# A recurrent layer: half of its products as bf16 sums, the other products in one bank

## The chip, the cores and the metric

One core of one Trainium2 chip runs the kernel; the other cores are idle. The metric is device time of the whole program in microseconds, the median of several runs. TensorE (PE in the profile; PEld is its weight load) multiplies matrices into PSUM; VectorE (DVE), ScalarE (ACT) and GpSimd (POOL) do the rest, and SyncE (SP) issues most DMAs. The clock granted to TensorE is 1.000 over the whole profiled run.

## The reference

A gated recurrent layer walks over 512 steps of a sequence, for a batch of 8, with 512 inputs and 512 state units, all in fp32. Its result is added to the input.

```python
def step(h, x_t):
    fused = jax.nn.sigmoid(jnp.concatenate([x_t, h], axis=-1) @ w_W + w_b)
    hidden_state, output_state = jnp.split(fused, 2, axis=-1)
    memory_state = x_t @ wx_W + wx_b + hidden_state * (h @ wh_W + wh_b)
    h_new = output_state * h + (1.0 - output_state) * jnp.tanh(memory_state)
    return (h_new, h_new)
_, hs = jax.lax.scan(step, h0, xT)
return x + jnp.swapaxes(hs, 0, 1)
```

Below, r is `hidden_state`, z is `output_state`, and hh is `h @ wh_W + wh_b`. Each step needs three products of h (r, z, hh) and three of x (r, z, and the memory's own). The products of x do not depend on h and can be made ahead; those of h make up a loop that no step can leave.

## The kernel before

**Layout.** The 512 units are cut into 4 chunks of 128 for the contraction (index `k`) and into 4 quarters for the output (index `j`). A product of h has 8 columns of state (stationary; 32 are loaded, of which the 8 rows of the current step are used) and streams a weight slice. Quarter j of the output goes to partitions 32j to 32j+31 of a PSUM tile, so four products stand side by side. The output columns are again cut into two halves: half A is chunks 0 and 1 of the next state, half B is chunks 2 and 3.

**Steps and groups.** `GS = 4` steps form a group. The rows 8s to 8s+7 of each 32 belong to step s of the group, and the x products of all four steps are made at once. PSUM tiles exist twice, one set for each group in turn. Weights and states are fp32; an fp32 product is two TensorE instructions, each with its weight load.

**Recurrent products.** Three tiles hold them: `A` with 192 columns (hh, z and r of half A), `B` with 128 (r and hh of half B), `C` with 64 (z of half B). `ORDER = "A0 B0 A1 A2 A3 B1 B2 B3 C0 C1 C2 C3"` is the order on TensorE; the digit is the chunk of h. Bank A is complete first, so that half A can be worked on while B and C are still being written.

**x products.** From group 4 on, pairs of groups are computed with a seven-product scheme (`products`, `weight_sum`, `x_sum`), which trades an eighth of the multiplications for sums on VectorE, ScalarE and GpSimd. A piece of it follows the recurrent products in each step (`take(later, 1)`), ahead of the next step's products. The first groups use plain products (`prefill`). `spread` copies the finished x part of r, z and hh into the banks of the next group (ScalarE), and `turn_x` transposes the memory's own x part into `md1` (VectorE). The x parts already hold the biases.

**Half A, then half B.** The instructions are put on their queues in the order of the program text (a manual schedule). On VectorE, for half A: a transpose of r, of hh and of z, a very short memset that waits for the second of these, a scan `m = r * hh + x` for each of the two chunks (`memory`), and, after the transposes of r and hh of half B, the two updates (`update`, also a scan). ScalarE does sigmoid of r, sigmoid of -z, and a tanh for each chunk in between. The scan of an update works on three cells for each element of h: the old h in slot 0, tanh in slot 1, and in slot 2 again the old h, in whose place the new tile gets the new one; factors 0, -1 and sigmoid(-z) make h + (1 - z)(tanh - h) of them. A copy of the new h into slot 0 (`act(("h", ...))`) prepares the next step. The first product of the next step (A0) waits for the first update of half A, A1 for the second, A2 and A3 for those of half B.

**Output.** GpSimd adds x and the new state into `ot` (16 steps), half B first, and SP stores 256 KB every 16 steps; the last 16 steps leave in two stores, the last of 4 steps.

**Waits.** They are set by the framework from tiles and regions; `declare_no_dep` takes some away that are implied by others, `add_manual_dep` adds some.

Names the prediction uses: `mm` (L193) makes all matmuls, so all of them show as L194; `act` (L223) makes all activations (L224); transposes of r and z are L406, of hh L422; all scans are L390; additions of the output are L558.

Of the kernel before, what the change touches and what calls it, by code (L numbers as in the profile page):

```python
# [11 lines left out]
PSUM = bass.MemoryType.PSUM  # L12

# [4 lines left out]
HU = 64  # L18

DVE_FILL = 23
IDLE = 3
LAST = 4
SYNC = mybir.DependencyInfo(mybir.DependencyClass.Sync, mybir.DependencyReason.DATA)

ORDER = "A0 B0 A1 A2 A3 B1 B2 B3 C0 C1 C2 C3"

FIRST = "A0 x A1 x A2 x A3 B0 B1 B2 B3 C0 C1 C2 C3"

BANKS = {"A": 192, "B": 128, "C": 64}

HALF = 192

WIDE = 384

SUMS = ((2,), (2,), (2, 1), (2, 1), (1,), (1, 3), (3,), (3, 3))

Q01, Q23 = slice(0, 64), slice(64, 128)

COLS = slice(64, 448)

XP = {"A": slice(0, 192), "X": slice(192, 320), "C": slice(320, 384), "B": slice(384, 512)}
# [3 lines left out]
def tile_cond_rnn_residual(  # L47
# [5 lines left out]
    wa_d: bass.AP,  # L53
    wb_d: bass.AP,
    wb3_d: bass.AP,
# [4 lines left out]

# [13 lines left out]

# [47 lines left out]

# [8 lines left out]

    wa = const.tile([P, NQ, NQ, 192], F32, name="wa")
    for k in range(NQ):
        nc.sync.dma_start(out=wa[:, k], in_=wa_d[k])
    wb = const.tile([P, NQ, NQ, 192], F32, name="wb")
    nc.sync.dma_start(out=wb[:, :3], in_=wb_d)
    nc.sync.dma_start(out=wb[:, 3], in_=wb3_d)

    def wh(bank, k, j):
        return wa[:, k, j] if bank == "A" else wb[:, k, j, {"C": slice(0, 64), "B": slice(64, 192)}[bank]]  # L140
# [3 lines left out]
    def pair(n, name, rows, slots):  # L144

        return const.tile([P, 2, rows, slots], F32, name=name).rearrange("p c n s -> p n c s")

    NH = 2 * GS  # L150
    hT = [[pair(n, f"hT{n}{i}", 32, 3) for i in range(NH)] for n in "AB"]

    md0 = [[pair(n, f"md0{n}{i}", 32, 2) for i in range(2)] for n in "AB"]
    md1 = [[pair(n, f"md1{n}{i}", 32, 2) for i in range(2)] for n in "AB"]
    hd0 = [[pair(n, f"hd0{n}{i}", B, 3) for i in range(2)] for n in "AB"]
# [3 lines left out]
    nc.vector.memset(none, 0.0)  # L159

# [6 lines left out]
    for n, t_ in enumerate(hd0[0] + hd0[1] + md0[0] + md0[1] + hT[0] + hT[1]):  # L167
        (nc.vector if n < DVE_FILL else nc.gpsimd).memset(t_, 0.0)
    for t_ in hd0[0] + hd0[1]:
        nc.gpsimd.memset(t_[:, :, :, 1], -1.0)  # L170
    idle = const.tile([P, IDLE], F32, name="idle")

    tw = [const.tile([P, 2, 2, WIDE], F32, name=f"tw{n}") for n in range(4)]
    sx = [[const.tile([P, 2, GS * B], F32, name=f"sx{n}{q}") for q in range(2)] for n in range(4)]
    step_bias = const.tile([P, HALF], F32, name="stepbias")
    xs = [const.tile([P, 512], F32, name=f"xs{n}") for n in range(2)]
    u2 = const.tile([P, WIDE], F32, name="u2")
    u3 = const.tile([P, WIDE], F32, name="u3")
    both = const.tile([P, WIDE], F32, name="both")

    def state(hf, i, slot=2):

        s = i % GS
        return hT[hf][i % NH][:, B * s : B * s + B, :, slot]

    ctx.enter_context(tc.manual_schedule())
    banks = [
        {n: psum.tile([P, w], F32, name=f"{n}{q}") for n, w in BANKS.items()}
        for q in range(2)
    ]  # L190
    xps = [psum.tile([P, 512], F32, name=f"xp{q}") for q in range(2)]

    def mm(out_, lhsT, rhs, start=False):  # L193
        nc.tensor.matmul(  # L194
            out_, lhsT, rhs, start=start, stop=False, skip_group_check=True
        )


    for t_ in list(banks[0].values()) + list(banks[1].values()):
# [10 lines left out]
    for t_ in xs:  # L210
        for c_ in (slice(0, 64), slice(448, 512)):
            nc.gpsimd.tensor_copy(t_[:, c_], bias[:, c_])
    for hf in range(2):
        for slot in (0, 2):
            nc.vector.tensor_copy(
                state(hf, 0, slot), hin[:, 2 * hf : 2 * hf + 2].rearrange("p c b -> p b c")
            )

    written = {}

# [6 lines left out]

    def seed(g):  # L230

        nc.scalar.copy(xps[g % 2][:, COLS], bias[:, COLS])

    def prefill(g):

        c, t0 = divmod(g * GS, TC)
        for k in range(NQ):
            for j in range(NQ):
                mm(
                    xps[g % 2][32 * j : 32 * j + 32, 64:448],  # L240
                    x_of(c, k, t0, GS),
                    wx[:, k, j, :],
                )
            yield

    def prefill_two():
        yield from prefill(2)
        yield from prefill(3)

    def source(g):  # L250

        return xs[g % 2] if g else xps[0]

    def spread(g, names):

        for n in names:
            nc.scalar.copy(banks[g % 2][n], source(g)[:, XP[n]])

    def turn_x(g, e):

        c0 = XP["X"].start + 32 * e
        nc.vector.transpose(md1[e // 2][g % 2][:, :, e % 2, 1], source(g)[:, c0 : c0 + 32])

    def wx_of(kh, nh):
        return wx[:, 2 * kh : 2 * kh + 2, 2 * nh : 2 * nh + 2]

    def x_half(o, n, kh):

        return x_of(o // 2, slice(2 * kh, 2 * kh + 2), 8 * (o % 2) + GS * n, GS)

    def weight_sum(n, k=slice(0, 2), j=slice(0, 2)):

        a, b = [
            (wx_of(0, 1), wx_of(0, 0)),
            (wx_of(1, 1), tw[0]),
            (wx_of(1, 1), wx_of(0, 1)),
            (wx_of(1, 0), tw[1]),
        ][n]
        at = (slice(0, P), k, j)
        nc.vector.tensor_tensor(tw[n][at], a[at], b[at], ALU.subtract)  # L280

    def x_sum(o, n):

        t_ = [q[o % 2] for q in sx]
        a, b, op = [
            (x_half(o, 1, 0), x_half(o, 1, 1), ALU.add),
            (t_[0], x_half(o, 0, 0), ALU.subtract),
            (x_half(o, 0, 0), x_half(o, 1, 0), ALU.subtract),
            (x_half(o, 0, 1), t_[1], ALU.subtract),
        ][n]  # L290
        nc.gpsimd.tensor_tensor(t_[n], a, b, op)

    def products(o):

        t_ = [q[o % 2] for q in sx]
        p1 = (0, x_half(o, 0, 0), wx_of(0, 0))
        p2 = (0, x_half(o, 0, 1), wx_of(1, 0))
        p3 = (0, t_[3], wx_of(1, 1))
        p4 = (1, x_half(o, 1, 1), tw[3])
        p6 = (0, t_[1], tw[1])  # L300
        p7 = (1, t_[2], tw[2])

# [55 lines left out]
    for e in range(NQ):  # L358
        turn_x(0, e)
# [297 lines left out]
```

## Time and profile before

| | |
|---|---|
| Median of 3 runs | 1662.64 us (1661.88 to 1666.37) |
| Profiled execution, first to last instruction | 1659.2 us |
| Median less that span | 3.4 us |
| PE busy | 1647.1 us, 99% |
| PEld busy | 1484.3 us, 89% |
| DVE busy | 1298.5 us, 78% |
| ACT busy | 1106.9 us, 67% |
| POOL busy | 325.6 us, 20% |
| Chain that ended last | PE 98%, DMA 1%, DVE 1% |
| PEld waiting for the update of half A (hTA) | 107.1 us in 379 waits |
| DVE waiting for bank A | 199.3 us in 384 waits |

How to read it: rows of the groups give line, engine, operation, tile written <- tiles read, shape and count, then busy time in us and the mean in ns, then idle time of that engine just before, with what ended most of it. Rows in order of time give start, length and the same names; idle time stands in brackets. Rows of the chain give start, length, engine, tile and count. Matmul ends are modelled, and busy time of several engines overlaps.

### The profile page before, as it was taken

How to read it: one execution, taken by the hardware profiler on the slowest of the kernel's cores; microseconds unless marked ns; L12 is line 12 of the kernel's file. 1: busy time of each engine (PE TensorE's matmuls, PEld its weight loads, DVE VectorE, ACT ScalarE, POOL GpSimd, SP SyncE). 2: the span in 40 equal slices, each digit the busy share in tenths (PEclk: the TensorE clock that was granted, in tenths of full speed). 3: DMA queues.
4: the chain of work that ended last, by engine and by line, in shares of the span. 5: the costliest groups of instructions: out<-in, count | busy, mean ns of one | idle time of the engine just before them, and what ended most of it. 6: DMA issues, size and time to landing. Idle time of an engine off the chain costs nothing.

```text
span 1659.2 us, 126037 instructions
## 1 busy us (share of the span) xinstructions
PE 1647.1 (99%) x54254; PEld 1484.3 (89%) x54254; DVE 1298.5 (78%) x9702; ACT 1106.9 (67%) x5884; POOL 325.6 (20%) x1284
## 2 busy tenths in 40 slices
PE   8999999999999999999999999999999999999998
PEld 5899999999999888899999999988899999999997
DVE  6877777777777777777777777777777777777776
ACT  4666666666666666666666666666666666666665
POOL 2221121211211212112112121121121211211211
PEclk9999999999999999999999999999999999999999
DMA  4000000000000000000000000000000000000000
GB/s 180 17 5 18 17 18 18 17 6 18 17 17 18 5 18 18 18 18 5 18 18 18 18 12 10 18 17 18 18 5 18 17 18 18 5 17 11 11 11 10
DMA packets 11512, 31.16 MB, mean 19 GB/s; under 512 B 1220, under 2 KB 1732, under 8 KB 10824
## 3 DMA queue, kind: packets, MB, share of 16 engines
q1 hardware_dynamic: 10800, 22.94, 4.0%
q8 instruction: 424, 6.95, 1.8%
q14 instruction: 136, 1.11, 0.2%
q10 hardware_dynamic: 152, 0.16, 0.0%
HBM read 14.70 MB, written 8.39 MB: 14 GB/s over the span
## 4 chain that ended last, share of the span: by engine, by line
PE 98%; DMA 1%; DVE 1%; issue 0%; ACT 0%; SPq 0%
PE A L194 40%; PE B L194 26%; PE xp L194 18%; PE C L194 13%; DMA wb<-in_wb_dram 1%; DMA wx<-in_wx_dram 0%; DVE tr L406 0%; DVE m L390 0%; DVE tz L406 0%; DVE hTA L390 0%; DVE md1A L422 0%; DVE md1B L422 0%; ACT hTB L224 0%; SPq L130 0%; DVE hTB L390 0%
## 5 line engine op out<-in xcount | busy, mean ns | idle before, releaser
L194 PE MATMUL A<-wa,hTA 128*32 128x192 f32 x8176 | 555.5, 327 | 2.7 <-DVE hTA L390 2.7
L194 PE MATMUL B<-wb,hTA 128*32 128x128 f32 x8192 | 453.0, 273 | 0.9 <-DMA wb<-in_wb_dram 0.9
L194 PE MATMUL A<-wa,hTB 128*32 128x192 f32 x8176 | 446.6, 326 | 0.0
L194 PEld LDWEIGHTS A<-wa,hTA 128*32 128x32 f32 x8176 | 290.7, 122 | 128.4 <-DVE hTA L390 107.1
L558 POOL TENSOR_TENSOR ot<-xin,hTB 128x16 f32<-128x16 f32 x503 | 125.6, 250 | 1292.4 <-DVE hTB L390 1281.8
L194 PEld LDWEIGHTS B<-wb,hTA 128*32 128x32 f32 x8192 | 346.8, 122 | 10.8 <-DMA wb<-in_wb_dram 1.3
L194 PE MATMUL B<-wb,hTB 128*32 128x128 f32 x8192 | 338.6, 273 | 0.1
L194 PEld LDWEIGHTS A<-wa,hTB 128*32 128x32 f32 x8176 | 324.3, 122 | 15.5 <-DVE hTB L390 0.3
L224 ACT ACTIVATE md0A<-tr 128x16 f32<-128x16 f32 x512 | 112.3, 219 | 314.4 <-DVE tr L406 314.4
L406 DVE STREAM_TRANSPOSE tr<-A 128x64 f32<-128x64 f32 x511 | 127.7, 250 | 214.3 <-PE A L194 199.3
L194 PE MATMUL xp<-tw,sx 128*32 128x384 f32 x1984 | 274.2, 406 | 0.3 <-issue 0.3
L194 PEld LDWEIGHTS B<-wb,hTB 128*32 128x32 f32 x8192 | 261.1, 122 | 0.4 <-DMA wb<-in_wb_dram 0.4
L390 DVE TENSOR_TENSOR_SCAN hTB<-hd0B,hTB 128x24 f32<-128x24 f32 x1024 | 157.8, 195 | 100.5 <-ACT hTB L224 100.5
L194 PE MATMUL C<-wb,hTB 128*32 128x64 f32 x8192 | 230.0, 219 | 0.1
L194 PE MATMUL C<-wb,hTA 128*32 128x64 f32 x8192 | 229.1, 219 | 0.0
L194 PE MATMUL xp<-wx,xin 128*32 128x384 f32 x1056 | 210.1, 486 | 0.0
L194 PEld LDWEIGHTS C<-wb,hTA 128*32 128x32 f32 x8192 | 206.6, 122 | 0.0
L390 DVE TENSOR_TENSOR_SCAN hTA<-hd0A,hTA 128x24 f32<-128x24 f32 x1024 | 190.9, 186 | 0.0
L194 PEld LDWEIGHTS C<-wb,hTB 128*32 128x32 f32 x8192 | 179.5, 122 | 0.6 <-issue 0.4
L224 ACT ACTIVATE hd0B<-tz 128x16 f32<-128x16 f32 x512 | 115.7, 226 | 94.8 <-DVE tz L406 94.8
L224 ACT ACTIVATE hTB<-hTB 128x16 f32<-128x16 f32 x512 | 120.1, 235 | 79.2 <-DVE hTB L390 70.3
L224 ACT ACTIVATE hTA<-m 128x8 f32<-128x8 f32 x1024 | 160.8, 206 | 2.5
(98 smaller groups left out, 2710.0 us busy)
## 6 DMA issues: line engine op xcount, KB each, us to landing
xin<-in_x_dram SPq DMA_DIRECT2D x31, 256.0 KB, 3.3
out_dram<-ot SPq DMA_DIRECT2D x31, 256.0 KB, 2.1
wx<-in_wx_dram SPq DMA_DIRECT2D x4, 768.0 KB, 7.1
wa<-in_wa_dram SPq DMA_DIRECT2D x4, 384.0 KB, 9.1
wb<-in_wb_dram SPq DMA_DIRECT2D x1, 1152.0 KB
wb<-in_wb_dram SPq DMA_DIRECT2D x1, 384.0 KB, 11.2
out_dram<-ot SPq DMA_DIRECT2D x1, 192.0 KB, 2.1
head<-in_xh_dram ACTq DMA_DIRECT2D x1, 144.0 KB, 5.0
```

The source lines that it names most:

```text
L194: nc.tensor.matmul(out_, lhsT, rhs, start=start, stop=False, skip_group_check=True)
L224: inst = nc.scalar.activation(out_, in_, func, **kw).ins
L390: return nc.vector.tensor_tensor_scan(*[t_[:, :, c_].rearrange("p n c s -> p (n c s)") for t_ in (out_, d0, d1)], 0.0, ALU.mult, ALU.add,).ins
L406: inst = nc.vector.transpose(t_.rearrange("p c n -> p (c n)"), raw[n][hf]).ins
L558: return engine.tensor_tensor(ot[:, t, 2 * hf : 2 * hf + 2, :].rearrange("p c n -> p n c"), x_of(c, slice(2 * hf, 2 * hf + 2), t, 1).rearr ...
```

## The change

**Recurrent products.** One fp32 tile `M` of 256 columns holds hh, r and z of half A and r of half B. `COLS` cuts it: M0 and M1 (chunks 0, 1 of h) write all 256 columns, A2 and A3 the columns of hh and r of A, R2 and R3 those of z of A and r of B. A second tile `Z` of 128 columns holds hh and z of half B. Its products are in bf16: each fp32 weight is split before the loop into three bf16 numbers whose sum is exact (`split`), and so is each new h (`first_piece`, a ScalarE copy whose upper 16 bits serve as the first piece; `other_pieces`, two GpSimd subtractions). The three pieces of h are 24 stationary columns, the three of the weights are three products, so that 3 x 3 partial products come out as 24 rows, summed over the weights' pieces in PSUM. The three rows of each element, and a fourth with the bias, are summed later: for hh by a longer scan (five cells for each element, `SL = 5`), for z by a `tensor_reduce`. Z has a tile for each step in turn.

**Order.** `"M0 M1 Z0 A2 A3 R2 R3 Z1 Z2 Z3"`, then one chunk of the plain x products of the group after next.

**x side.** `products` and all its sums are gone; `prefill` is used throughout, 384 columns for one chunk in each step. Two groups are made ahead of the loop. `spread` copies two pieces of 128 columns for a group, `turn_x` transposes directly from `xp`.

**Others.** The copy of half B's h into slot 0 and both output additions are on GpSimd, in the order: pieces of A, addition of A, pieces of B, copy of B, addition of B. The last 16 steps leave in one store. The weights are loaded in other pieces (wzf, then wm).

```diff
-ORDER = "A0 B0 A1 A2 A3 B1 B2 B3 C0 C1 C2 C3"
-BANKS = {"A": 192, "B": 128, "C": 64}
+ORDER = "M0 M1 Z0 A2 A3 R2 R3 Z1 Z2 Z3"
+COLS = {"M": slice(0, 256), "A": slice(0, 128), "R": slice(128, 256)}
+HA, RA, ZA, RB = (slice(HU * n, HU * n + HU) for n in range(4))
+    banks = [psum.tile([P, 256], F32, name=f"M{q}") for q in range(2)]
+    zbanks = [psum.tile([P, 128], F32, name=f"Z{q}") for q in range(2)]
+    def first_piece(hf, i):
+        first_of[hf] = act(("p", hf, i % 2), pieces[hf][i % 2][:, :, :B], state(hf, i), AF.Copy)
+        after_products(first_of[hf], hf, i)
+
+    def other_pieces(hf, i):
+        t_ = pieces[hf][i % 2]
+        hi = t_.rearrange("p c n -> p (c n)").bitcast(BF16).rearrange("p (c n) -> p c n", c=2)[:, :, 1::2]
+        d = nc.gpsimd.tensor_tensor(t_[:, :, B : 2 * B], state(hf, i), high(hf, i), ALU.subtract).ins
+        after_products(d, hf, i)
+        e = nc.gpsimd.tensor_tensor(
+            t_[:, :, 2 * B : 3 * B], t_[:, :, B : 2 * B], hi[:, :, B : 2 * B], ALU.subtract
+        ).ins
+        after_products(e, hf, i)
+        tc.add_manual_dep(e, first_of[hf].name, SYNC)
+    def split(k):
+        w = wzf[:, k]
+        t_ = work.tile([P, NQ, 128], F32, tag="split", name=f"split{k}")
+        nc.scalar.copy(wzp[:, k, :, 0], w)
+        nc.vector.tensor_tensor(t_, w, wzp[:, k, :, 0], ALU.subtract)
+        nc.scalar.copy(wzp[:, k, :, 1], t_)
+        nc.vector.tensor_tensor(wzp[:, k, :, 2], t_, wzp[:, k, :, 1], ALU.subtract)
+        for n in ORDER.split():
+            bank, k = n[0], int(n[1])
+            if bank != "Z":
+                hs = hT[k // 2][i % NH][:, k % 2, :, 2]
+                for j in range(NQ):
+                    mm(ps[32 * j : 32 * j + 32, COLS[bank]], hs, wm[:, k, j, COLS[bank]])
+                continue
+            hf, q = divmod(k, 2)
+            hs = pieces[hf][i % 2].rearrange("p c n -> p (c n)").bitcast(BF16)
+            hs = hs.rearrange("p (c n) -> p c n", c=2)[:, q, 1 : 2 * ROWS : 2]
+            for p in range(NP):
+                for j in range(NQ):
+                    inst = mm(pz[32 * j : 32 * j + ROWS, :], hs, wzp[:, k, j, p], start=k == p == 0)
...
+        if g in later:
+            take(later[g], 1)
...
+        tr = turned("rA", RA)
+        act(("rA", g % 2, s), a0[:, :, rows, 1], tr, AF.Sigmoid)
+        h_done = nc.vector.transpose(a1[:, :, :, 0], ps[:, HA]).ins
+        tz = turned("zA", ZA)
+        act(("zc", 0, i % 2), hd0[0][i % 2][:, :, :, 2], tz, AF.Sigmoid, scale=-1.0)
+        inst = nc.vector.memset(idle[:, :1], 0.0).ins
+        tc.add_manual_dep(inst, h_done.name, SYNC)
+        scan_m(0, 0)
+        tr = turned("rB", RB)
+        scan_m(0, 1)
+        tanh(0, 0)
+        act(("rB", g % 2, s), b0[:, :, rows, SL - 1], tr, AF.Sigmoid)
+        tanh(0, 1)
+        nc.vector.transpose(b1[:, :2, rows, : SL - 1].rearrange("p c n s -> p c s n"), pz[:, :HU])
+        update(0, 0)
+        z_done = nc.vector.transpose(b1[:, 2:, rows, : SL - 1].rearrange("p c n s -> p c s n"), pz[:, HU:]).ins
+        tc.add_manual_dep(z_done, pool_done[i].name, SYNC)
+        update(0, 1)
+        if not last:
+            first_piece(0, i + 1)
+            other_pieces(0, i + 1)
+        scan_m(1, 0)
+        tanh(1, 0)
+        nc.vector.tensor_reduce(zB, b1[:, 2:, rows], mybir.AxisListType.X, ALU.add)
+        act(("zc", 1, i % 2), hd0[1][i % 2][:, :, :, 2], zB, AF.Sigmoid, scale=-1.0)
+        scan_m(1, 1)
+        tanh(1, 1)
+        update(1, 0)
+        update(1, 1)
+        if s == 0 and g + 1 < NG:
+            turn_x(g + 1)
+        if s in (1, 2) and g + 1 < NG:
+            spread(g + 1, "AR"[s - 1])
...
+            again(0, i + 1)
+            first_piece(1, i + 1)
+            add(0, nc.gpsimd)
+            other_pieces(1, i + 1)
+            again(1, i + 1)
+            add(1, nc.gpsimd)
+        if s == 3 and g + 3 < NG:
+            seed(g + 3)
```

`again` copies the new h into slot 0, on ScalarE for half A and on GpSimd for half B.

More of the change, by code (lines that the diff above doesn't have):

```diff
@@ L209, in tile_cond_rnn_residual, with after_products @@
     nc.vector.tensor_copy(bias, xps[0])
[L210 to L217, printed above, removed]
-    written = {}
+    for t_ in zbanks:
+        nc.vector.tensor_copy(t_[:, :HU], bias[:, 448:])
+    written = {}
+    read = set()
+    def after_products(inst, hf, i):
+        key = f"z{hf}{i % 2}"
+        if key in read:
+            tc.declare_no_dep(inst, group=key, reason="ordered through VectorE")
     def act(key, out_, in_, func, **kw):
@@ L345, in take @@
             n = None if n is None else n - 1
[L347 to L362 removed]
+    def split(k):
[5 more added lines that the diff above has]
+        nc.vector.tensor_tensor(wzp[:, k, :, 2], t_, wzp[:, k, :, 1], ALU.subtract)
+    seed(0)
+    take(prefill(0))
+    seed(1)
+    take(prefill(1))
+    spread(0, "M")
+    turn_x(0)
+    seed(2)
+    for k in range(NQ):
+        split(k)
+    later = {}
     for i in range(T):
@@ L563, in add @@
             ).ins
[L565 to L583 removed]
+        last = i == T - 1
```

435 lines of the change are left out of this document (103 added, 332 removed).

## The prediction

> **What bounds the kernel now.** I read the page first, then the chain that ended last, then the order of time in one late step.
>
> ```profile
> span 1659.2 us, 126037 instructions
> PE 1647.1 (99%) x54254; PEld 1484.3 (89%) x54254; DVE 1298.5 (78%) x9702; ACT 1106.9 (67%) x5884; POOL 325.6 (20%) x1284
> ```
> ```profile
> 803.27 0.65 PE xp L194 x8
> 803.92 0.33 PE A L194 x8
> 804.24 0.22 PE B L194 x8
> 804.46 0.97 PE A L194 x24
> 805.43 0.66 PE B L194 x24
> 806.09 0.45 PE C L194 x32
> ```
> In mid-run the chain is PE alone, and this step takes 3.28 us (803.27 to 806.54): 2.63 us of recurrent products, 0.65 us of x products. The paces behind it: 40 ns per instruction at 192 columns (0.97/24), 27.5 at 128 (0.66/24), 14 at 64 (0.45/32); an fp32 product is two instructions.
>
> ```profile
> 35.17 0.25 DVE L406 STREAM_TRANSPOSE tr<-A 128x64 f32<-128x64 f32 x1 [0.71 <-PE A L194]
> 1654.18 0.25 DVE L406 STREAM_TRANSPOSE tr<-A 128x64 f32<-128x64 f32 x1 [0.95 <-PE A L194]
> ```
> These are the first transposes of steps 4 and 511: 1619.0 us over 507 steps, 3.193 us a step, so the x share is 0.56 on average.
>
> The last steps have no x products left, and there the other limit can be seen bare: the loop through VectorE and ScalarE. First the chain view, then the order of time.
>
> ```profile
> 1649.29 0.55 PE A L194 x8
> 1649.84 0.22 PE B L194 x8
> 1650.06 1.02 PE A L194 x24
> ```
> ```profile
> 1651.10 0.25 DVE L406 STREAM_TRANSPOSE tr<-A 128x64 f32<-128x64 f32 x1 [0.94 <-PE A L194]
> ...
> 1651.40 0.21 DVE L406 STREAM_TRANSPOSE tz<-A 128x64 f32<-128x64 f32 x1
> ...
> 1651.64 0.28 DVE L390 TENSOR_TENSOR_SCAN m<-md0A,md1A 128x16 f32<-128x16 f32 x2
> ...
> 1651.83 0.23 DVE L406 STREAM_TRANSPOSE tr<-B 128x64 f32<-128x64 f32 x1
> 1651.86 0.31 ACT L224 ACTIVATE hTA<-m 128x8 f32<-128x8 f32 x2
> 1651.98 0.21 DVE L422 STREAM_TRANSPOSE md1B<-B 128x64 f32<-128x64 f32 x1
> 1652.09 0.22 ACT L224 ACTIVATE md0B<-tr 128x16 f32<-128x16 f32 x1
> 1652.11 0.20 DVE L390 TENSOR_TENSOR_SCAN hTA<-hd0A,hTA 128x24 f32<-128x24 f32 x1
> ...
> 1652.37 0.19 PEld L194 LDWEIGHTS A<-wa,hTA 128*32 128x32 f32 x8 [0.38 <-DVE hTA L390]
> ...
> 1652.38 0.17 DVE L390 TENSOR_TENSOR_SCAN hTA<-hd0A,hTA 128x24 f32<-128x24 f32 x1
> 1652.47 0.25 DVE L390 TENSOR_TENSOR_SCAN m<-md0B,md1B 128x16 f32<-128x16 f32 x2
> ```
> The loop has two arcs. On PE, from the first load of h of half A to the transpose of r of A: 1649.29 to 1651.10, 1.81 us. Its streams are 32 instructions at 40.4 ns and 8 at 27.5, 1.51 us, so 0.30 us is loading, draining and handing over. On the others, from that transpose back to PE's load: 1.27 us. Together 3.08 us, only 0.11 under the average step. PE bounds the kernel, and the loop lies just behind it. Only products before bank A is complete (A0 B0 A1 A2 A3) are in the loop; the other B, C and x products run in the shadow of the 1.27 us.
>
> **PE's own work.** Bank M has 4 chunks x 4 quarters x 256 columns: 32 fp32 instructions of 256 columns' worth, at 54 ns (40.4 x 256/192), 1.73 us. The Z products are 12 rounds of 4 bf16 instructions with 128 columns.
>
> ```profile
> L194 PE MATMUL A<-none 128*128 128x192 bf16 x2 | 0.7, 345 | 2.1 <-DVE none L159 2.1
> ```
> Two such bf16 products stand in the program and two in the row: one instruction each. One pass over 128 columns is the stream of a C product, two over 64; I take C's 14 ns, so Z0 is 12 x 14 = 0.17 us and Z1 to Z3 0.51. The row is the nearest I have; no steady bf16 row exists, and the bounds are half of it and twice (see the rivals). The plain x side is one 384-column chunk in every step, 0.65. Sum: 1.73 + 0.68 + 0.65 = 3.06, against 3.19. If PE stayed the bound, this would give 0.13 us a step. It does not stay the bound.
>
> **What the one bank does.** Before, the transpose of r of A waits for bank A alone, with B and C still to be written. Now hh, r and z of A and r of B lie in one bank. The question is whether a read of r of A must wait only for its own columns (complete after A3) or for everything written to that bank (R3).
>
> ```profile
> 12.53 0.33 ACT L257 COPY A<-xp 128x192 f32<-128x192 f32 x1
> 12.89 0.32 DVE L262 STREAM_TRANSPOSE md1A<-xp 128x32 f32<-128x32 f32 x2 [2.25 <-ACT A L257]
> ```
> Here both engines read xp, ScalarE columns 0 to 191, VectorE 192 to 255: no column in common, and yet VectorE sat idle until ScalarE's copy was over (12.86). Waits are set by bank. So I take it that the first transpose waits for R3. The Trainium skill, PSUM — Partial Sum Buffer, section "PSUM bank collisions raise a hardware error", says the same more widely: a matmul writing a bank and a VectorE read of it in the same 32 partitions collide at disjoint columns too. By that rule the column case below falls away; the row shows it for two readers only.
>
> **The new loop.** PE arc: M0 and M1, 16 x 54 ns = 0.86; Z0 0.17; A2 A3 and R2 R3, 32 x 27.5 ns = 0.88; with the 0.30 of hand-overs 2.21 us, where it was 1.81. The 0.40 more is R2 and R3 (0.44) and small differences, and all of it is in the loop.
>
> Other arc, counted from the transpose of r of A. The order up to the first update is the old one with one exchange: r of B is transposed between the two m scans, and the transpose of hh of B now reads bank Z (done 0.51 after R3, long before it is wanted at 0.88). So the first update starts at 1.01 and PE's load at 1.27 as before. The second update waits for the second tanh, which now stands behind r of B on ScalarE.
>
> ```profile
> 906.33 0.23 ACT L224 ACTIVATE hTB<-hTB 128x16 f32<-128x16 f32 x1 [0.15 <-DVE hTB L390]
> 906.47 0.32 ACT L257 COPY A<-xs 128x192 f32<-128x192 f32 x1
> ```
> r of B was transposed at 0.73 and stands one scan (0.10) earlier now, 0.63; its sigmoid starts 0.26 later (1651.83 to 1652.09), 0.89; ScalarE takes the next 0.14 behind it, 1.03; a tanh is followed by its update 0.25 later (1651.86 to 1652.11): 1.28, as before (1652.38).
>
> 2.21 + 1.27 = 3.48 us. PE has only 3.06 us of work, and Z1 to Z3 and x (1.16) end before the new load (1.27), so they are hidden.
>
> **The pieces for Z0.** A wait that did not exist: Z0 stands third in PE's order, in front of A2, and needs three pieces of half A of h: a ScalarE copy and two GpSimd subtractions one behind the other. All of PE queues behind them.
>
> ```profile
> 804.03 0.31 DVE L390 TENSOR_TENSOR_SCAN hTB<-hd0B,hTB 128x24 f32<-128x24 f32 x2 [0.20 <-ACT hTB L224]
> 804.42 0.25 POOL L558 TENSOR_TENSOR ot<-xin,hTB 128x16 f32<-128x16 f32 x1 [2.38 <-DVE hTB L390]
> ```
> ```profile
> 24.81 0.52 DVE L280 TENSOR_TENSOR tw<-wx 128x384 f32<-128x384 f32 x1
> 24.86 0.57 POOL L558 TENSOR_TENSOR ot<-head,hTB 128x16 f32<-128x16 f32 x1 [3.07 <-DVE hTB L390]
> ```
> GpSimd starts 0.08 after an update ends and takes 0.25 for 16 elements; it took 0.57 beside a VectorE operation on two SBUF tensors. The second update ends at 1.28 + 0.17 = 1.45; subtractions from 1.53 to 2.03, two hand-overs of 0.07, ready at 2.17. PE wants Z0 at 1.27 + 0.03 + 0.86 = 2.16. So even at the free price nothing is left, and the scans of half B, each on two SBUF tensors, run exactly then. They are far shorter than the 0.52 us operation, so I take 0.035 for each subtraction, near the free row: 0.07 us of stall, 3.55 us a step. Ends: 0 (3.48) and 2 x 0.32 (4.12).
>
> **Half B.** Its update is wanted by A2 at 2.16 + 0.17 + 0.07 = 2.40. Second update 1.28, a scan 0.09 later, 1.37 (1652.38 to 1652.47). That scan has 40 elements now; two of 16 take 0.25, so 0.15 until the next operation is my estimate. Then the sum of the z pieces, which has no row; priced like a transpose and its sigmoid (0.26), the sigmoid starts at 1.37 + 0.15 + 0.26 = 1.78, the update 0.25 later at 2.03, the load 0.26 later at 2.29. It is 0.1 early; a reduction slower by 0.2 would cost 0.1, a faster one gains nothing. The second half's tanh stands behind that sigmoid, 0.14 later, and A3 wants it 0.22 later than A2. What follows per step or per group (the copies of h, the spread, the seed at 0.48 us, the turned x, the two output additions) falls behind the last update, some 1 us ahead of the next first transpose; GpSimd has six operations of 0.25, 1.5 us, in 3.5.
>
> **Start and end.** SP's queue loads 3 MB of recurrent weights as before, in eight pieces for six; a step cannot start before the last of them, then or now. Four weight splits stand on ScalarE and VectorE ahead of step 0.
>
> ```profile
> L232 ACT COPY xp<-bias 128x384 f32<-128x384 f32 x3 | 1.4, 479 | 4.6 <-DVE bias L209 4.6
> 17.01 0.25 DVE L406 STREAM_TRANSPOSE tr<-xp 128x64 f32<-128x64 f32 x1 [3.62 <-PE xp L194]
> ```
> A split of 512 elements is two copies (479 x 512/384 = 0.64, taken as 0.6) and two subtractions (0.52 x 512/384 = 0.69, the row at 24.81): 2.6 us, about 2 where neighbours overlap, 8 in all from 13.1, so step 0 starts near 21.5 instead of 17.0. But steps 0 to 3 no longer carry x work for two groups (35.17 - 17.01 = 18.2 us; now 14.2 and about 1 of settling): step 4 at 36.7. The end, 5.0 us from the last first transpose, grows by a later half B and by one 256 KB store in place of 64 KB: 6.2.
>
> Sum: 36.7 + 507 x 3.55 + 6.2 = 1842.8 us of span. The profiled span stands 3.4 under the median of the runs (1659.2 to 1662.64), so **1846 us**, 11% slower. Of the 183 us, 147 are the 3.48 us loop (0.29 x 507), 35 the pieces.
>
> **The rivals.**
> Columns, not banks (not slower): the first transpose starts after A3. The PE arc loses 0.44, but z of A, second in VectorE's queue behind it, still waits for R3, 0.44 after, instead of being taken at 0.30, and moves all behind it by 0.14: 3.48 - 0.44 + 0.14 = 3.18; 36.7 + 1612.3 + 6.2 + 3.4 = 1659 us, no change. Pieces are then no tighter than above. It decides if the transpose of r starts before R2's stream is over. Against it speaks the xp row. Chance 0.09, split over faster and same.
>
> GpSimd slowed in full: both subtractions at 0.57. Step 4.12: 507 x 4.12 + 46.3 = 2135 us. For it, the 0.57 row; against it, that scans of 16 to 40 elements are not 0.5 us long. Full 0.07; half of it (3.8, 1973 us) 0.10.
>
> bf16 instructions at twice C's pace, 28 ns: Z0 costs 0.17 more in the loop, and Z1 to Z3 with x last 1.01 + 0.65 = 1.66 from R3's stream; PE is wanted about 1.55 after it (1.27 + 0.03 + the 0.25 to the transpose), so 0.11 more: 3.48 + 0.28 = 3.76, 1953 us. The C row, 14 ns for the same stream, speaks against it. Chance 0.08. The Trainium skill, TensorE: Matmul & The Clock Gate, section "Wait — 56ns, not 53.3ns?", has a floor of about 25 ns between starts of small matmuls. By that, as an estimate, Z0 would be 0.30 and the step 3.61, some 1877 us; the trace has 14 ns with four quarters side by side, and I go by it.
>
> PE stays the bound (3.06 a step, 1598 us): the loop would have to be 0.4 shorter than its rows. Chance 0.02.
>
> **How the numbers follow.** Forecast 1846 with 0.64, its own range 1790 (no stall, and 0.04 of shorter hand-overs) to 1900. Left out of 1780 to 1985: columns and PE-bound, 0.11, below, and the full GpSimd price, 0.07, above. Faster takes PE-bound and half of the column case, same the rest of it; 5 us, 0.3%, is about what the measurement can tell: faster 0.06, same 0.05, slower 0.89.
>
> **What would show it.** Right: the transpose of r waits for PE's R products; the load of M on hTA shows idle of some 0.1 to 0.4 us in every step; PE's busy share falls below nine tenths; chain shares of VectorE and ScalarE appear; Z0 waits for GpSimd. Wrong: first transpose before R3 is over; PE still 98% of the chain; Z rows above 14 ns per instruction; or GpSimd far from 0.25.

## The result

The changed kernel takes 1804.5 us in the median (1803.98 to 1804.84, four runs), the one before 1662.62 us beside it: ratio 1.085, 95% interval 1.084 to 1.087. The forecast was 1846 us, its range 1780 to 1985.

From the page of the kernel after: its span, the busy time of each engine, the queue that brings instructions (packets, MB, share), and the engines' shares of the chain that ended last.

```profile
span 1802.8 us, 125916 instructions
...
PE 1687.8 (94%) x53258; PEld 1123.5 (62%) x53258; DVE 1203.0 (67%) x8495; ACT 1054.2 (58%) x6025; POOL 719.2 (40%) x3600
...
q8 instruction: 416, 6.82, 1.7%
...
PE 61%; DVE 35%; issue 2%; DMA 1%; ACT 0%; SPq 0%; POOL 0%; DVEq 0%; ACTq 0%
```

Before, PE alone was 98% of the chain. Now VectorE has a third of it. PE is still shown as 94% busy, but its ends are modelled and its matmuls overlap, so this figure says little here; the idle time of the weight loads tells more. The groups of the kernel after:

```profile
L148 PEld LDWEIGHTS M<-wm,hTA 128*32 128x32 f32 x8192 | 241.8, 125 | 527.4 <-DVE hTA L286 452.4
...
L292 DVE STREAM_TRANSPOSE trA<-M 128x64 f32<-128x64 f32 x512 | 128.0, 250 | 507.8 <-PE M L148 507.8
...
L148 PEld LDWEIGHTS <-pcA 128*24 128x24 bf16 x12288 | 249.9, 92 | 130.5 <-POOL pcA L191 128.0
```

The first two rows are the loop with nothing to cover it: PE's loads stand idle 452.4 us for the update of half A (0.9 us a step), and VectorE's first transpose waits 507.8 us for PE (1.0 us a step). Before, these waits were 107.1 and 199.3 us. The third row is Z0's loads waiting for the pieces that GpSimd makes, 128.0 us. The chain through one step shows the two arcs one behind the other:

```profile
903.06 0.25 DVE trA L292
...
904.33 1.09 PE M L148 x16
905.41 0.17 PE Z L148 x12
905.58 0.92 PE M L148 x32
906.50 0.02 issue
906.52 0.25 DVE trA L292
```

From the transpose of r of A to PE's load is 1.27 us (903.06 to 904.33), from there back to the next transpose 2.19 us (to 906.52), 3.46 us together, where the average step before was 3.193. Over the whole run the first transposes and the weight splits ahead of them give the same sum (rows in order of time, kernel after):

```profile
17.33 0.69 DVE L236 TENSOR_TENSOR split<-wzf,wzp 128x512 f32<-128x512 f32 x1 [1.21 <-ACT wzp L235]
...
24.65 0.69 DVE L238 TENSOR_TENSOR wzp<-split,wzp 128x512 bf16<-128x512 f32 x1 [0.69 <-ACT wzp L237]
...
25.25 0.24 DVE L292 STREAM_TRANSPOSE trA<-M 128x64 f32<-128x64 f32 x1
...
40.16 0.25 DVE L292 STREAM_TRANSPOSE trA<-M 128x64 f32<-128x64 f32 x1 [1.10 <-PE M L148]
...
1797.05 0.25 DVE L292 STREAM_TRANSPOSE trA<-M 128x64 f32<-128x64 f32 x1 [1.10 <-PE M L148]
```

Steps 4 to 511: 1756.9 us over 507, 3.465 us each. The 0.272 us a step more than before make 138 of the 142 us that were lost.

### The profile page after: what moved, and what is told of

The parts are those of the page before. It is cut to its first block, busy times and chain, and to the rows that moved or that the text cites. A ratio compares the mean times of both kernels' runs of the same rounds, so it can differ in the third digit from the quotient of the medians.

```text
span 1802.8 us, 125916 instructions
## 1 busy us (share of the span) xinstructions
PE 1687.8 (94%) x53258; PEld 1123.5 (62%) x53258; DVE 1203.0 (67%) x8495; ACT 1054.2 (58%) x6025; POOL 719.2 (40%) x3600
## 4 chain that ended last, share of the span: by engine, by line
PE 61%; DVE 35%; issue 2%; DMA 1%; ACT 0%; SPq 0%; POOL 0%; DVEq 0%; ACTq 0%
PE M L148 57%; DVE mA L286 8%; DVE trA L292 7%; DVE md1B L333 5%; PE Z L148 5%; DVE trB L292 4%; DVE mdA L322 4%; DVE tzA L292 4%; DVE hTA L286 3%; DMA wzf<-in_wz_dram 1%; DVE idle L325 0%; DMA xin<-in_x_dram 0%; SPq L85 0%; DVE split L236 0%; ACT wzp L237 0%
## 5 line engine op out<-in xcount | busy, mean ns | idle before, releaser
L148 PE MATMUL M<-wm,hTA 128*32 128x256 f32 x8192 | 556.8, 389 | 100.6 <-DVE hTA L286 100.6
L148 PEld LDWEIGHTS M<-wm,hTA 128*32 128x32 f32 x8192 | 241.8, 125 | 527.4 <-DVE hTA L286 452.4
L148 PE MATMUL M<-wm,hTB 128*32 128x128 f32 x16384 | 540.8, 273 | 0.0
L292 DVE STREAM_TRANSPOSE trA<-M 128x64 f32<-128x64 f32 x512 | 128.0, 250 | 507.8 <-PE M L148 507.8
L189 POOL TENSOR_TENSOR pcA<-hTA 128x16 f32<-128x16 f32 x512 | 110.9, 217 | 889.5 <-DVE hTA L286 882.2
L148 PEld LDWEIGHTS M<-wm,hTB 128*32 128x32 f32 x16384 | 436.4, 122 | 0.0
L148 PE MATMUL Z<-wzp,pcA 128*24 128x128 bf16 x12288 | 359.4, 219 | 1.7 <-DVE wzp L238 1.0
L148 PEld LDWEIGHTS <-pcA 128*24 128x24 bf16 x12288 | 249.9, 92 | 130.5 <-POOL pcA L191 128.0
L148 PE MATMUL Z<-wzp,pcB 128*24 128x128 bf16 x12288 | 265.8, 219 | 2.9 <-ACT wzp L237 1.9
L286 DVE TENSOR_TENSOR_SCAN mB<-md0B,md1B 128x40 f32<-128x40 f32 x1024 | 229.0, 224 | 0.0
L173 ACT ACTIVATE hTB<-mB 128x8 f32<-128x8 f32 x1024 | 223.4, 218 | 0.4 <-DVE mB L286 0.4
L335 DVE STREAM_TRANSPOSE md1B<-Z 128x64 f32<-128x64 f32 x512 | 141.4, 276 | 0.0
L333 DVE STREAM_TRANSPOSE md1B<-Z 128x64 f32<-128x64 f32 x512 | 139.6, 273 | 0.0
## 6 DMA issues: line engine op xcount, KB each, us to landing
xin<-in_x_dram SPq DMA_DIRECT2D x1, 128.0 KB, 7.3
```

The lines of the kernel that those rows point to most:

```text
L148: return nc.tensor.matmul(out_, lhsT, rhs, start=start, stop=False, skip_group_check=True).ins
L173: inst = nc.scalar.activation(out_, in_, func, **kw).ins
L189: d = nc.gpsimd.tensor_tensor(t_[:, :, B : 2 * B], state(hf, i), high(hf, i), ALU.subtract).ins
L286: return nc.vector.tensor_tensor_scan(*[t_.rearrange("p n s -> p (n s)") for t_ in (out_, d0, d1)], 0.0, ALU.mult, ALU.add).ins
L292: nc.vector.transpose(t_.rearrange("p c n -> p (c n)"), ps[:, cols])
L333: nc.vector.transpose(b1[:, :2, rows, : SL - 1].rearrange("p c n s -> p c s n"), pz[:, :HU])
```

## The experiments

Theory: the loop with the 256-column bank in it sets the time, because the first transpose waits for R3. Rivals: PE's own work, x included; the pieces on GpSimd; half B.

**The x products.** Left out from the third group on, with their two lines:

```diff
-        if g in later:
-            take(later[g], 1)
```

> The x products are left out from the third group on (the banks get biases alone, so the states are others): 0.65 us of PE work less in each step. Theory (the loop bounds, x lies in the shadow of VectorE's arc): no change, step 3.46, median 1795 to 1808. Rival (PE's work is the bound, 94% busy): 0.65 x 507 = 330 us less, about 1475.

Measured 1803.79 us. A fifth of PE's work (0.65 us a step) is worth less than 1 us: it lies wholly in the shadow of VectorE's arc. PE's busy share falls from 94% to 76% and the time stays. PE's amount of work is not the bound.

**The bank.** The same columns in two tiles, so that r and hh of A wait for their own products alone:

```diff
-ORDER = "M0 M1 Z0 A2 A3 R2 R3 Z1 Z2 Z3"
+ORDER = "A0 R0 A1 R1 Z0 A2 A3 R2 R3 Z1 Z2 Z3"
-COLS = {"M": slice(0, 256), "A": slice(0, 128), "R": slice(128, 256)}
+COLS = {"A": slice(0, 128), "R": slice(128, 256)}
-    banks = [psum.tile([P, 256], F32, name=f"M{q}") for q in range(2)]
+    banks = [
+        {n: psum.tile([P, c_.stop - c_.start], F32, name=f"{n}{q}") for n, c_ in COLS.items()}
+        for q in range(2)
+    ]
```

> One part undone: the bank M is cut into two tiles, A with hh and r of half A, R with z of half A and r of half B; order A0 R0 A1 R1 Z0 A2 A3 R2 R3 Z1 Z2 Z3, so PE has the same instructions' worth of columns at the same places. Theory (a read waits for the whole bank): the first transpose now waits for A3, 0.44 us sooner after the load of M, and z of A, second behind it, still waits for R3, which gives 0.14 back: step 3.47 - 0.30 = 3.16 to 3.18 us, median 1650 to 1660. Rival (waits go by columns and the loss is elsewhere, in Z0 or in PE's work): the step stays at 3.47, median about 1804.

Measured 1806.47 us (1800.07 to 1811.99), ratio 1.087 (1.083 to 1.091): taken alone, that is the rival's number, and my forecast missed by 150 us. But the steps are of unequal length. First transposes of four steps, then two weight loads, from the order of time of this kernel:

```profile
896.70 0.25 DVE L302 STREAM_TRANSPOSE trA<-A 128x64 f32<-128x64 f32 x1 [0.24 <-PE A L157]
900.61 0.25 DVE L302 STREAM_TRANSPOSE trA<-A 128x64 f32<-128x64 f32 x1 [1.47 <-PE A L157]
903.73 0.25 DVE L302 STREAM_TRANSPOSE trA<-A 128x64 f32<-128x64 f32 x1 [0.68 <-PE A L157]
906.84 0.25 DVE L302 STREAM_TRANSPOSE trA<-A 128x64 f32<-128x64 f32 x1 [0.67 <-PE A L157]
```
```profile
898.23 0.12 PEld L157 LDWEIGHTS xp<-wx,xin 128*32 128x32 f32 x3 [0.73 <-issue]
...
898.55 0.17 PEld L157 LDWEIGHTS A<-wm,hTA 128*32 128x32 f32 x4 [0.17 <-issue]
```

One step takes 3.91 us, the two behind it 3.12 and 3.11. In the long step the loads stand still for 0.73 and 0.17 us, and wait for nothing that the profile shows ("issue"). Such gaps are mostly 3.5 to 4.0 us apart, at any place in the order, and now and then one is missing. Where none falls, the step is 0.35 us shorter than with one bank, as the bank theory has it. The edit had a side effect: M0 and M1 were cut in two, so a step has 120 pairs of load and matmul instead of 104. (Of the 104, the bf16 products are 48, for a third of the recurrent columns.)

**The instructions.** The next kernel keeps the one bank and only issues more instructions: M0, M1 and the x products in two halves each, with the same columns in the same banks, 128 pairs a step.

```diff
-ORDER = "M0 M1 Z0 A2 A3 R2 R3 Z1 Z2 Z3"
+ORDER = "A0 R0 A1 R1 Z0 A2 A3 R2 R3 Z1 Z2 Z3"
-                mm(xps[g % 2][32 * j : 32 * j + 32, XCOLS], x_of(c, k, t0, GS), wx[:, k, j, :])
+                for u in range(2):
+                    mm(
+                        xps[g % 2][32 * j : 32 * j + 32, 64 + 192 * u : 256 + 192 * u],
+                        x_of(c, k, t0, GS),
+                        wx[:, k, j, 192 * u : 192 * u + 192],
+                    )
```

> The changed kernel with its one bank; M0 and M1 are issued as two products of 128 columns each, and each x product as two of 192: the same columns, 256 instructions a step instead of 208. Theory (instructions come at 14.4 ns on average): 3.69 us a step, median 1890 to 1950, with idle time of PE that no engine ends. Rival (only streamed columns count): 3.47 us, 1804.

Measured 1897.91 us, ratio 1.144. From its page, and from its waits (the loads of the Z products; total, count, longest):

```profile
span 1900.9 us, 150492 instructions
...
PE 1742.6 (92%) x65546; PEld 1515.7 (80%) x65546; DVE 1207.1 (63%) x8495; ACT 1055.8 (56%) x6025; POOL 720.1 (38%) x3600
...
q8 instruction: 512, 8.39, 1.8%
```
```profile
PEld L148 <- issue: 149.3, 263, 1.5
```

Not one column more, and 93 us slower than the kernel after. Its loads stand idle at "issue" for 178.3 us in all, against 12.9 there. The instructions of PE and PEld together, 131,092, are 256 for each packet of q8; so are the 106,516 of the kernel after for its 416. Span over instructions gives 14.5 ns here, 14.6 in the two-bank kernel (1797.6 us, 122,904), 16.9 in the kernel after, 15.3 in the one before. Both kernels that stall at "issue" run at the same pace per instruction, whatever their loop. That TensorE got no more than one instruction in 14.5 ns on average in them, though a burst of bf16 products runs at 14 ns per pair, is what the runs show. That the fetch through q8 is the cause is inferred, from its packets and from the distance of the gaps: 256 instructions at 14.6 ns are 3.7 us. The Trainium skill, Runtime: NRT & Kernel Launch, section "Instruction fetch mechanics", has blocks of 256 instructions, with which the packets agree. It also has the fetch hidden behind a slower issue; if the gaps are the fetch, these two runs do not bear that out.

**The bank again, without that side effect.** To keep 104 pairs, the products of the third weight piece of Z were left out (its sums are a little less exact), once with two banks and once with one:

```diff
-            for p in range(NP):
+            for p in range(NP - 1):
```

> The two banks of the first experiment again, with the third bf16 piece of the weights left out of the products of Z (so hh and z of half B are a little less exact): 104 TensorE pairs of load and product in a step instead of 120. In the first experiment the undisturbed steps took 3.11 us and the others up to 4.1, with idle time of PE that no engine ends (issue). Theory (bank plus instruction supply: 240 instructions a step came at 14.4 ns each): 208 instructions need 3.00 us, so the loop shows, 3.11 less 0.06 for a shorter Z0: step 3.05 to 3.11, median 1594 to 1625. Rival (supply is not the cause, the cut of the bank does nothing): 3.40 as with one bank, median 1772. If the bank was wrong and only instructions count: 3.00, 1570.

> The changed kernel with its one bank, the third piece of the weights left out of the products of Z: the companion of the run with two banks. Theory (the loop through the bank bounds): only Z0's share counts, 0.06 us a step, 3.40, median 1770 to 1778; Z1 to Z3, 0.17 us less, lie in the shadow. Rival (PE's work or its instructions bound): 0.22 us a step, median about 1692.

Two banks: 1611.85 us, ratio 0.972 (0.970 to 0.973) to the kernel before. One bank: 1791.18 us, ratio 1.080 (1.078 to 1.081). One step of the two-bank kernel in order of time:

```profile
904.23 0.25 DVE L302 STREAM_TRANSPOSE trA<-A 128x64 f32<-128x64 f32 x1 [0.19 <-PE A L157]
...
905.58 0.19 PEld L157 LDWEIGHTS A<-wm,hTA 128*32 128x32 f32 x8 [0.69 <-DVE hTA L296]
...
906.32 0.35 DVE L296 TENSOR_TENSOR_SCAN hTB<-hd0B,hTB 128x24 f32<-128x24 f32 x2
...
906.58 0.40 PEld L157 LDWEIGHTS A<-wm,hTB 128*32 128x32 f32 x16
...
907.31 0.25 DVE L302 STREAM_TRANSPOSE trA<-A 128x64 f32<-128x64 f32 x1 [0.64 <-PE A L157]
```

The arcs are now 1.35 us (904.23 to 905.58) and 1.73 us (to 907.31), the step 3.08. PE's arc is 0.46 us shorter than in the kernel after: R2 and R3 (0.44) are out of the loop, and Z0 is 0.06 shorter, which shows in part. VectorE's arc is 0.08 longer, since the transpose of z of A waits for the second bank (the column rival had put 0.14 for this). In the chain that ended last PE has 97% again, so PE's own work and the loop are nearly level here. The one-bank run lies 13 us above its forecast. Its A2 loads come 1.01 us after M0's, 0.26 behind the start of half B's update, as in the kernels below that wait for that update; its trace shows no idle time there, since Z0's loads stand just ahead. The cut of the bank is worth 179 us between these two runs, which also differ in 16 pairs; the shared bank was therefore more than the whole loss, and this version beats both kernels. The third weight piece, 16 pairs a step, is worth 13 us with one bank and 195 us with two: the instructions count only where the loop leaves them no time.

**The pieces on GpSimd.** A copy of 16 elements that nobody reads, first between the two subtractions, then ahead of the first:

```diff
         d = nc.gpsimd.tensor_tensor(t_[:, :, B : 2 * B], state(hf, i), high(hf, i), ALU.subtract).ins
         after_products(d, hf, i)
+        nc.gpsimd.tensor_copy(spare, state(hf, i))
```

> One more GpSimd copy of 16 elements stands between the two subtractions of each half, its result unused. Theory (the pieces for Z0 are ready just when PE wants them, with no slack): Z0 and all behind it come 0.15 to 0.25 us later, step 3.62 to 3.72, median 1885 to 1935. Rival (slack of a GpSimd operation or more): 1804.

Measured 1804.44 us, as without it, but this did not test the slack. The second subtraction waits for the result of the first, which comes about 0.1 us behind its end, and the added copy, which waits for nothing new, fitted into that gap: the three began at 904.62, 904.78 and 904.95, the two without it at 904.60 and 904.92. So the other place:

```diff
+        nc.gpsimd.tensor_copy(spare, state(hf, i))
         d = nc.gpsimd.tensor_tensor(t_[:, :, B : 2 * B], state(hf, i), high(hf, i), ALU.subtract).ins
```

> One GpSimd operation more (a copy of 16 elements nobody reads) ahead of the first subtraction of each half; all else is the changed kernel. In the changed kernel the subtractions take 0.22 us each and Z0's loads follow 0.25 us behind their release, while PE's stream ran on without a gap. If the third piece is ready just when PE wants Z0 (slack near 0), some 0.16 to 0.22 us more on GpSimd stand in the loop: a step of 3.62 to 3.68 us, 1885 to 1915 us. If there are two tenths of slack, 1804 us as before.

Measured 1850.29 us. The rows of the pieces, first of the kernel after, then of this one:

```profile
904.33 0.62 PEld L148 LDWEIGHTS M<-wm,hTA 128*32 128x32 f32 x16 [0.88 <-DVE hTA L286]
...
904.60 0.21 POOL L189 TENSOR_TENSOR pcA<-hTA 128x16 f32<-128x16 f32 x1 [1.70 <-DVE hTA L286]
...
904.92 0.21 POOL L191 TENSOR_TENSOR pcA<-pcA 128x16 f32<-128x16 f32 x1
...
905.07 0.35 DVE L286 TENSOR_TENSOR_SCAN hTB<-hd0B,hTB 128x24 f32<-128x24 f32 x2
...
905.19 0.21 PEld L148 LDWEIGHTS <-pcA 128*24 128x24 bf16 x12 [0.25 <-POOL pcA L191]
...
905.35 0.85 PEld L148 LDWEIGHTS M<-wm,hTB 128*32 128x32 f32 x32
```
```profile
904.98 0.61 PEld L149 LDWEIGHTS M<-wm,hTA 128*32 128x32 f32 x16 [0.89 <-DVE hTA L288]
...
905.70 0.21 POOL L193 TENSOR_TENSOR pcA<-pcA 128x16 f32<-128x16 f32 x1
...
905.96 0.17 PEld L149 LDWEIGHTS <-pcA 128*24 128x24 bf16 x12 [0.36 <-POOL pcA L193]
```

Counted from M0's load, the last subtraction begins at 0.72 instead of 0.59, 0.13 later, and the time grows by 45.8 us, 0.09 a step. So the pieces of the kernel after have about 0.04 us to spare (0.13 less 0.09), and what goes beyond that is paid. The time lies between the two forecasts, in neither: the near-zero slack was right, but the copy, 0.20 us long, put off what follows by 0.13 only.

**Z0 out of the loop, and half B.** Only the order of the kernel after:

```diff
-ORDER = "M0 M1 Z0 A2 A3 R2 R3 Z1 Z2 Z3"
+ORDER = "M0 M1 A2 A3 R2 R3 Z0 Z1 Z2 Z3"
```

> Only the order on PE is changed: Z0 goes behind R3 (M0 M1 A2 A3 R2 R3 Z0 Z1 Z2 Z3). Theory: Z0's 0.17 us lies in the loop, but it covers half B, whose first update ends so that A2's load can start 1.00 us after M0's load, while M0 and M1 stream until 0.90: about 0.1 of the 0.17 comes back as a wait of PE for hTB, step 3.39 to 3.43, median 1765 to 1787. Rival (half B is early enough): the whole 0.17 is gained, step 3.30, median 1718. If Z0's place costs nothing: 1804.

Measured 1791.05 us, ratio 1.077 (1.075 to 1.079): of Z0's 0.17 us only 0.03 was gained, a little less than the theory had (1765 to 1787). The rest became a new wait, a group row of this kernel:

```profile
L148 PEld LDWEIGHTS M<-wm,hTB 128*32 128x32 f32 x16384 | 430.7, 123 | 201.7 <-DVE hTB L286 199.2
```

The loads of A2 and what follows stand idle 0.39 us in each step for the update of half B. A2's load comes 1.00 us after M0's, in this kernel (904.09 and 903.09) as in the two-bank one with two pieces (906.58 and 905.58), where Z0 still covers the wait. The limit behind the loop is thus half B's chain. Four attempts to get under it, all with two banks and two weight pieces; the first with z of B transposed and summed early, and Z0 late:

```diff
-ORDER = "A0 R0 A1 R1 Z0 A2 A3 R2 R3 Z1 Z2 Z3"
+ORDER = "A0 A1 R0 R1 A2 A3 R2 R3 Z0 Z1 Z2 Z3"
-        nc.vector.transpose(b1[:, :2, rows, : SL - 1].rearrange("p c n s -> p c s n"), pz[:, :HU])
-        update(0, 0)
         z_done = nc.vector.transpose(b1[:, 2:, rows, : SL - 1].rearrange("p c n s -> p c s n"), pz[:, HU:]).ins
         tc.add_manual_dep(z_done, pool_done[i].name, SYNC)
+        update(0, 0)
+        nc.vector.transpose(b1[:, :2, rows, : SL - 1].rearrange("p c n s -> p c s n"), pz[:, :HU])
         update(0, 1)
+        nc.vector.tensor_reduce(zB, b1[:, 2:, rows], mybir.AxisListType.X, ALU.add)
...
         scan_m(1, 0)
-        tanh(1, 0)
-        nc.vector.tensor_reduce(zB, b1[:, 2:, rows], mybir.AxisListType.X, ALU.add)
         act(("zc", 1, i % 2), hd0[1][i % 2][:, :, :, 2], zB, AF.Sigmoid, scale=-1.0)
+        tanh(1, 0)
```

> Two banks, two pieces of the weights (the third left out), Z0 behind R3, R0 and R1 between A1 and A2, and on VectorE the z of half B transposed ahead of its hh and summed ahead of half B's first scan. Theory: A0 A1 and R0 R1 stream 0.88 us, A2 finds half B ready at about 0.87, A3 ends, with hand-overs 0.28, 1.60 after the first load; the other arc is 1.27 and 0.14 for z of A: 3.01, and the instructions need 3.00: step 3.00 to 3.10, median 1570 to 1620, faster than the kernel before. Rival (half B is later than that): A2 waits 0.1 to 0.2, step 3.10 to 3.25, median 1620 to 1695.

Measured 1618.72 us, ratio 0.976. The number lies at the upper end of the theory's range, but the theory's mechanism failed: A2's load is at 1.02 and not at 0.87. What z gained, the m scan and the tanh of half B lost, and the update now waits for the tanh. Then Z0 late alone:

```diff
-ORDER = "A0 R0 A1 R1 Z0 A2 A3 R2 R3 Z1 Z2 Z3"
+ORDER = "A0 R0 A1 R1 A2 A3 R2 R3 Z0 Z1 Z2 Z3"
```

> The kernel with two tiles and two weight pieces, only the order changed: Z0 behind R3 with Z1 to Z3. Theory: the second update of half A and the update of half B bound it (A2's load about 1.00 us after A0's), and Z0 lay inside that wait; so the step stays at 3.08 to 3.10 us: 1605 to 1625 us. Rival: PE's own stream was the bound of that arc, and it loses Z0's 0.11 us: 1555 to 1570 us.

Measured 1612.85 us, as with Z0 early: PE's 0.11 us were free, half B sets A2 (its load now waits 0.17 us a step for half B and comes at 1.02). Then the first m scan of half B ahead of the second update of half A:

```diff
+        scan_m(1, 0)
         update(0, 1)
         if not last:
             first_piece(0, i + 1)
             other_pieces(0, i + 1)
-        scan_m(1, 0)
         tanh(1, 0)
```

> As the kernel with Z0 last, and in addition the first m scan of half B stands ahead of the second update of half A on VectorE. Half B's chain begins about 0.1 us earlier, so A2's load comes at about 0.90 instead of 1.00 us after A0's: PE's arc 1.63 instead of 1.73, with the other arc at 1.35 a step of 2.98 us: 1555 to 1580 us. TensorE's instructions (208 a step at 14.4 ns, 3.0 us) would then be the next limit: if they bind earlier, idle time on TensorE that ends at issue appears and the time lies between 1580 and 1612 us. If the second update of half A, now later, costs as much as half B gains: 1605 to 1625 us.

Measured 1655.07 us, ratio 0.997 (0.996 to 0.998): worse by 42 us, and no forecast had it. The waits of the loads for half B, in the kernel with Z0 last and then in this one, account for it; ScalarE shows why, in order of time:

```profile
PEld A L157 <- DVE hTB L296: 87.8, 505, 0.2
```
```profile
PEld A L157 <- DVE hTB L296: 130.5, 509, 0.4
```

```profile
906.59 0.19 PEld L157 LDWEIGHTS A<-wm,hTA 128*32 128x32 f32 x8 [0.58 <-DVE hTA L296]
...
906.94 0.23 ACT L182 ACTIVATE pcA<-hTA 128x16 f32<-128x16 f32 x1 [0.39 <-DVE hTA L296]
...
907.07 0.20 ACT L182 ACTIVATE hTB<-mB 128x8 f32<-128x8 f32 x1
...
907.41 0.35 DVE L296 TENSOR_TENSOR_SCAN hTB<-hd0B,hTB 128x24 f32<-128x24 f32 x2 [0.24 <-ACT hd0B L182]
```

The copy of the first piece waits for the second update, now 0.12 us later, and the tanh of half B stands behind it on ScalarE, so the scan done earlier was of no use. The update came 0.82 us after A0's load, where it had come at 0.76 with Z0 last and at 0.74 with Z0 early. Last, the whole beginning of half B ahead of update and copy:

```diff
-        update(0, 1)
-        if not last:
-            first_piece(0, i + 1)
-            other_pieces(0, i + 1)
         scan_m(1, 0)
         tanh(1, 0)
         nc.vector.tensor_reduce(zB, b1[:, 2:, rows], mybir.AxisListType.X, ALU.add)
         act(("zc", 1, i % 2), hd0[1][i % 2][:, :, :, 2], zB, AF.Sigmoid, scale=-1.0)
+        update(0, 1)
+        if not last:
+            first_piece(0, i + 1)
+            other_pieces(0, i + 1)
```

> As the kernel with Z0 last (1612.85 us), but the whole beginning of half B, its first m scan, its tanh, the sum of the z pieces and its sigmoid, stands ahead of the second update of half A on VectorE and ahead of the first piece of half A on ScalarE. In the kernel with the scan alone moved, ScalarE's copy of the first piece waited 0.13 us longer for the second update, and the tanh of half B stood behind it; half B's update came 0.82 instead of 0.74 us after A0's load. If that is the cause, half B's update now comes about 0.64 after A0's load and A2's load at 0.90 instead of 1.00; A1's load, now at 0.49, is 0.06 us late. Step 3.03 to 3.05 us: 1580 to 1597 us. If instead the late second update of half A costs through A1 itself, 1612 us or more; if it costs as in the kernel with the scan moved, 1640 to 1660 us.

Measured 1632.89 us, ratio 0.983 (0.981 to 0.984): 22 us better than the scan alone, 20 worse than none of it.

```profile
904.73 0.19 PEld L157 LDWEIGHTS A<-wm,hTA 128*32 128x32 f32 x8 [0.58 <-DVE hTA L296]
...
905.30 0.19 PEld L157 LDWEIGHTS A<-wm,hTA 128*32 128x32 f32 x8 [0.17 <-DVE hTA L296]
905.43 0.50 DVE L296 TENSOR_TENSOR_SCAN hTB<-hd0B,hTB 128x24 f32<-128x24 f32 x2
...
905.69 0.48 PEld L157 LDWEIGHTS A<-wm,hTB 128*32 128x32 f32 x16
```

Half B's update came at 0.70 and A2's load at 0.96, forecast 0.64 and 0.90, so that part worked by half, but A1's load stands at 0.57 instead of the forecast 0.49, since the second update began at 0.32, behind a scan and a sum; in the chain A1 takes 0.35 us where it took 0.22. The rival had it right: the second update of half A and the beginning of half B compete for VectorE, and both are wanted. How the 20 us divide between that wait and idle time at "issue", 21 us of which appear here and 7 in the kernel with Z0 last, is not settled. The kernels with two banks and two pieces in the old order on VectorE, Z0 early or last (1611.85 and 1612.85 us), stayed the fastest and are level.

## Why the prediction was right, and what was mis-sized

- **The bound before, and PE not staying it.** Right: without its x products the kernel after took the same time. That PE bounded the kernel before rests on its chain (98%); no run took work out of that kernel.
- **Waits set by the bank.** Right. The first transpose waited for R3 in each step, and with the bank cut it waited for A3 alone. Tile and bank were cut together in all runs, so they show that the wait goes beyond the columns read; whether its unit is the tile or the bank stays open. The Trainium skill, PSUM — Partial Sum Buffer, section "PSUM bank collisions raise a hardware error", wants readers and writers of a bank kept apart whatever their columns; the waits of this kernel agree.
- **The new loop.** 2.21 + 1.27 = 3.48 us forecast, 2.19 + 1.27 and on average 3.465 measured. The 0.015 us are 7 us of time.
- **The signs.** The wait for the R products, VectorE in the chain and Z0's loads behind GpSimd came as named. Three were off: the loads of M stand idle 0.9 us a step where 0.1 to 0.4 was put (the loads run ahead of the products; PE's products stand idle 100.6 us there, 0.20 a step), PE's busy share is 94% and not below nine tenths, and ScalarE has 0% of the chain.
- **The pieces for Z0.** The mis-sized term: 0.07 us of stall a step, 35 us in all. In the chain Z0 follows M1 without a gap. The subtractions took 0.217 us in the mean (110.9 us over 512) where I had 0.25, and 0.035 more for neighbours on VectorE. No slowing shows beside scans of 16 to 40 elements, so the rivals with half and full price fall. That nothing was left behind the free price was right to a few hundredths: the forecast had the pieces ready at 2.17 and wanted at 2.16 after the first transpose, Z0's loads came at 2.13 (905.19 less 903.06), and the added copy found 0.04 us of slack. In part this is luck: in the chain Z0's products begin only at 2.35 (905.41), since M0 and M1 take 1.09 us and not 0.86 there, and that the loads are wanted some 0.2 ahead of the products was not in the sum.
- **bf16 pace.** 12 Z products took 0.17 us in the chain, 14 ns each, as taken from C. The floor of 25 ns of the Trainium skill (TensorE: Matmul & The Clock Gate, section "Wait — 56ns, not 53.3ns?") did not show there.
- **Half B.** Update forecast at 2.03 and A2's load at 2.29 after the first transpose, measured 2.01 and 2.29 (905.07, 905.35). The 0.1 us of earliness counted on the stall of Z0; without it 0.04 was left, and this is why taking Z0 away brought 0.03 and not 0.17.
- **Start and end.** The splits took 8.7 us for 8 (from ScalarE's first copy at 16.68 to 25.34) and began 3.6 us later than I put them, since ScalarE's spread ahead of them waited 4.2 us for x products on PE: step 0 at 25.25 for 21.5, step 4 at 40.16 for 36.7. From 11.68 to 14.87 the granted clock was 0.50, and four x products took 0.64 us where they took 0.32 before and after that stretch, so about 1.6 of these microseconds are the clock (half of 3.2, an estimate). In the kernel before, the clock was 1.00 throughout the start. The sum had no term for this, and no run shows what lowered the clock. The end took 5.75 us for 6.2, and the median lies 1.7 us above the span for 3.4.
- **The sum.** 1846.2 less 35.5 (pieces), less 7.4 (loop), plus 3.5 (start), less 0.5 (end), less 1.7 (span to median) is 1804.6.
- **A rival that was not named.** TensorE's instructions per step. The kernel before ran at 15.3 ns per instruction, within 6% of where the two other kernels stalled. It did not bind in the kernel after, but it set the time of the first experiment.

## What to carry over

Put into one bank only what is wanted at the same time: in these runs a reader of its first columns waits for the last write to any of them, and here 0.44 us of products that nobody was waiting for entered a loop of 3 us. Before taking work off the engine that is the bound, add up the loop behind it from bare steps (here at the end of the run), since it decides how much of the gain can be kept; and count the engine's instructions as well as its columns. When one queue item is moved, look at what stands behind the thing that waits for it, on every queue: half B's tanh stood behind a copy that waited for half A.

## What was not expected of the hardware

With 240 and 256 TensorE instructions a step, the time followed their number, 14.6 and 14.5 ns for each over the whole run, with idle gaps of the loads that wait for nothing in the profile: 158.6 us in 377 waits with 240, and 178.3 us with 256, most of it ahead of Z's loads (149.3 us in 263 waits, 0.57 in the mean). Kernels at 15.1 ns and above had few of them, 7 to 21 us in all. Short bursts go at twice that pace (a pair of load and matmul in 14 ns), so the limit shows only as an average over some microseconds, and the length of no single instruction gives it away.
